# The last 256 rows' recurrence by ScalarE's silu alone, last products by row tile, and new dates for the tail

## Chip, cores and metric

One core of one Trainium2 chip. The metric is the device time of one execution in microseconds (us), the median of several runs. TensorE (PE) multiplies matrices, VectorE (DVE) and GpSimd (POOL) do elementwise work, ScalarE (ACT) evaluates functions, and SyncE (SP) issues most transfers. Each engine works through its own instructions in order; an instruction waits at the head of its engine's queue until what it needs is there, and everything behind it waits too.

## The reference, cut to what matters

```
x = builder_state + mha(layernorm(builder_state), layernorm(base_state))   # 4096 rows, 3202 keys, 8 heads of 64
U = (layernorm(x) @ W_in.T + b_in) @ Bmat                                   # 64 states per row
def step(s, u_t):
    s = silu(s @ A.T) + u_t
    return (s, s)
_, states = scan(step, 0, U)                                                # 4096 steps, one behind the other
out = x + states @ Cmat + mod                                               # mod: one row, the same for all
```

All tensors are float32. The attention is nearly all of the arithmetic; the recurrence over 4096 rows is little work, but each step needs the one before.

## The kernel before

**Attention.** The 4096 query rows are cut into 8 blocks of 512, each with 4 pairs of heads and 2 halves of 256 queries: 64 units. A unit takes 13 steps over pairs of key chunks: scores on PE, exponentials ("weights") on ScalarE, sums of weights on VectorE, products with the values on PE. The last block takes its four first halves before its four second halves, so that the last unit ends the second half of the last 512 rows: the last 256 rows of the sequence.

**The recurrence.** It is contractive, so it is run in pieces from guessed starts, and the kernel compares at the end whether neighbouring pieces agree (to 2^-21 of the largest state); if any does not, a branch at the end (`attend`, line 2410 on) computes everything again step by step. For the rows before the last 256, two sweeps (`sweep`, line 1931) go over 256 pieces of 16 rows: sweep "a" during the last units of attention, from zero, to find starts, and sweep "b" after it, from those starts. One step of a sweep is: PE adds A times the last state to prepared terms (`z_`), ScalarE takes tanh of half of it (`tanh_`), VectorE multiplies (1 + tanh) with it (`h_`), which is twice its silu. All states are kept doubled, and the matrix `a_t` is halved for that (line 962). After each step of sweep b GpSimd adds the inputs (`states`), PE multiplies with Cmat (`products`, two parts of 256 columns), VectorE or ScalarE and GpSimd add the result to rows fetched from memory (`outputs`), and SP stores the rows; 16 steps store all but the last 256 rows.

**The last 256 rows** (`last_rows`, line 2078) come from the last unit. For two row tiles g of 128 rows: output products of the attention (`last_products`, into the PSUM pair `yb`), adding the residual (`l.x1`), mean and variance (`l.stats`), the power -1/2 on GpSimd (`l.factors`), normalising (`l.scaled`), transposing (`l.turn`, `l.copy`), the inputs U (`l.inputs`, `l.kept`); GpSimd adds the modulation row (`l.mod`). Then PE prepares the terms of all pieces (`l.terms`), and a chain of 20 steps follows (line 2191), 16 of them to warm up and 4 that count, each over 32 pieces of 4 rows in each of two halves of the partitions:

```
plan.add(("l.z", t), "PE", 150, partial(on_, t), [("l.h", t - 1)], d, [], [], "quarters")
plan.add(("l.tanh", t), "ACT", 180, partial(tanh_, t), [("l.z", t) if t else "l.terms"], d)
plan.add(("l.h", t), "DVE", 180, partial(h_, t), [("l.tanh", t)], d)
```

Line 1920 is every matmul with `a_t`, line 2158 the tanh of this chain, line 2161 its product, lines 1948 and 1955 tanh and product of the sweeps. After the chain `l.states` (line 2170) adds the inputs, `l.ys` (line 2212) multiplies with Cmat, `last_output` (line 2215) adds to the rows and issues the two last stores, one from SP and one from ScalarE.

**What sets the order.** Each piece of work is given to a planner (`Plan`, line 66) with its engine, an assumed cost in ns, the pieces it comes after, buffers it takes from rings and gives back, and a due date. `order` (line 131) plays the engines forward and, whenever one is free, takes the ready piece with the earliest date; that fixes each engine's instruction order before the kernel is built. The table `SHIFT` (line 93) moves the date of each sort of piece by so many steps of 2150 ns; a name with `.l` stands for that sort in the last two units. Pieces of cost 0 ("start", "py1", "close") only allocate buffers. PSUM here: the ring "s" has two slots of two banks, used by scores, then by the last unit's denominators (`pd_last`, line 1280), the terms of sweep b (`ready_scan`, line 2056) and one of the two pairs of output products (`ready_py`, line 2065).

Of the kernel before, what the change touches and what calls it, by code (L numbers as in the profile page):

```python
# [20 lines left out]
P = 128  # L21
# [54 lines left out]
class Plan:  # L76
# [16 lines left out]
    SHIFT = {  # L93
        "row.store": -0.5, "fold": 17, "rows.outs": 10.25, "heads": -12, "spread": 1.75, "query.flip": -11,
        "states": -5, "inverse": 14.75, "extra": 10, "scale": -55.75, "rest": 11, "row.mod": -20,
        "joined0": -6.25, "b": 1, "add.l": -23, "l.stats": -34.25, "last": -4.5, "base": -34.75,
        "inverse.l": -35, "rows.inputs": 6, "maximum": -13.75, "fall": -19, "query.stats": -4, "den": 6.5,
        "row.scaled": 16, "l.h": -11, "row.stats": -21.25, "rows.turn": 13, "query.scaled": 7.5, "l.mod": -0.5,
        "close": -10, "swap": -2.25, "products": -9, "gather.l": -8, "l.ys": -10, "fall.l": -2, "weights": -3.5,
        "rows.s": 2, "l.x1": 1, "l.kept": 6, "tq": 20, "l.store": -2, "row.move3": 11, "l.from": -5,  # L100
        "l.copy": -12, "l.states": -8, "l.turn": -4, "row.flip": 3.75, "swap.l": -18, "l.near": 4,
        "differ": 12.25, "row.load": 12, "add": -6, "rest.l": -8, "den.l": 11.5, "query.factors": 16,
        "sevenths": -6, "l.z": -2, "scale.l": -0.5, "outs": -3, "output": -12, "query.move3": 3, "number": 0.25,
        "l.inputs": -4, "q": -12, "sums": -4, "row.move2": 2, "row.move1": -0.25, "query.move0": 1.5,
        "stored1": -12, "counted": 1, "to": 12, "sums.l": 9, "row.kept": 8, "so": 10.75, "stored0": 2,
        "l.scaled": -0.25, "row.move0": 4, "rise": -1, "join": -12, "sample": 3.5, "l.idle": 11.75,
        "risen": -0.5, "c2": 1, "yb": 2, "query.load": 8, "query.move2": -4, "row.row": -0.5,
    }
# [112 lines left out]
def xattn_ssm_kernel(  # L221
# [1055 lines left out]
    def sums(w):  # L1277

        if w["last"]:
            w["pd"] = ps_s.tile([P, 2, 512], F32, tag="s", name="pd_last")[:, 0, :QU]  # L1280
            for b in range(2):
                for a in range(2):
                    nc.tensor.matmul(
                        w["pd"][a * HD : (a + 1) * HD],
                        ones,
                        rows_of(w, w["acc"][:, a, b, :], True),
                        start=(b == 0),
                        stop=(b == 1),
                        skip_group_check=True,
                    )  # L1290
            return
# [32 lines left out]
    def finish(w, i, d, plan):  # L1324
# [568 lines left out]
    def open_scan():  # L1893

        t = qp.tile([P, 2, QB], F32, tag="q", name="c2")[:, 0]
# [11 lines left out]
        for name, n in (  # L1907
            ("end0", NCK + 1), ("end1", NCK + 1), ("ul", PRE + 1 + P), ("hw", P), ("hl", P),
            ("sl", P + 1), ("df", NCK), ("thl", P // LT), ("st", P // LT),
            ("top", 1), ("bad", 1), ("badl", 1), ("badr", 1),  # L1910
        ):
            sv[name] = two[:, at_ : at_ + n]
            at_ += n
        assert at_ <= 1024

    def on_a(z, right, **how):

        for v in range(2):
            r = slice(v * NS, (v + 1) * NS)
            nc.tensor.matmul(z[r], a_t[r, r], right[r], stop=True, skip_group_check=True, **how)  # L1920

# [9 lines left out]
    def sweep(k, start, end, d=0, pace=0, after=()):  # L1931
# [32 lines left out]
        for j in range(L):  # L1964
# [100 lines left out]
    def ready_py():  # L2065

        yb = ps_s.tile([P, 2, H], F32, tag="s", name="py")
        sv["py"] = [None, [yb[:, v, :] for v in range(2)]]

# [8 lines left out]
    def last_rows(plan, d):  # L2078
# [75 lines left out]
        def on_(t):  # L2154
            on_a(z_(t), hs_(t - 1), start=False)

        def tanh_(t):
            nc.scalar.activation(sv["thl"], z_(t), AF.Tanh, scale=0.5)

        def h_(t):  # L2160
            nc.vector.scalar_tensor_tensor(hs_(t), sv["thl"], 1.0, z_(t), ALU.add, ALU.mult)

        def from_():

            nc.vector.tensor_tensor(
                sv["st"], sv["hw"][:, LT - 1 :: LT], sv["ul"][:, PRE :: LT][:, : P // LT], ALU.add
            )

        def states_():
            nc.vector.tensor_tensor(sv["sl"][:, 1:], sv["hl"], sv["ul"][:, PRE + 1 :], ALU.add)  # L2170
# [127 lines left out]
    def drain(plan):  # L2298
# [16 lines left out]
        for p in sweep("a", None, "end1", a0 + 1000, A_PACE, ["open"]):  # L2315
            plan.add(*p)
        plan.add("start", "DVE", 0, ready_scan, ["fetch", ("sums", n)], d - 2 * STEP, ["s"])
        plan.add("yb", "DVE", 0, ready_rows, [("den", n - 1, 1)], a0, ["m", "m"])
        plan.add("py1", "DVE", 0, ready_py, ["start", ("rise", n)], d, ["s"])
        for c in range(NC - 1):  # L2320
            i = units.index((NQB - 1, c, 1))
            plan.add(("last", c), "PE", 1900, partial(last_products, c),
                     ["yb"] + [("scale", i, t) for t in range(2) if ("scale", i, t) in plan.pieces] + ([("last", c - 1)] if c else []), d + 8 * STEP + c)
        for j in range(L):
# [245 lines left out]
    with tc.If(n > 0, label="general"):  # L2570
# [14 lines left out]
        with tc.For_i(0, 2 * P // LT, 1):  # L2585
            sl, th, h = sv["sl"], sv["thl"], sv["hw"][:, : P // LT]
            for j in range(LT):
# [70 lines left out]
```

## Time and profile before

| | |
|---|---|
| median of 3 runs | 1905.65 us (1905.32 to 1907.46) |
| the profiled execution | 1904.96 us, span 1903.1 us |
| granted TensorE clock, mean | 0.999 |
| last attention product ends | about 1847.5 us |
| sweep b, first tanh to last product | 1857.8 to 1889.9 us |
| chain over the last 256 rows | 1867.3 to 1894.9 us |
| last store issued | 1898.3 us |

A row of the timeline gives the start from the start of the span, the duration, engine, line of the kernel, operation, output and inputs, and, in square brackets, how long the engine had been idle before it and what ended that. Times are us. In rows that group instructions a mean in ns follows the busy time. PEld is the load of weights into TensorE.

### The profile page before, as it was taken

Reading aid. Unit: us, or ns where it says so; the run is one execution under the profiler, and the core shown is the slowest. Engines: PE = TensorE matmul, PEld = TensorE weight load, DVE = VectorE, ACT = ScalarE, POOL = GpSimd, SP = SyncE. Lnnn points to the kernel's source line nnn. Section 1 sums busy time; section 2 is a strip of 40 time slices with the busy share of each in tenths; the row PEclk is TensorE's granted clock in tenths of the full one; section 3 lists DMA queues with packets and bytes.
Section 4 is the critical chain, followed back from the end, with each engine's and each line's share of the span. In section 5 each row is a group of like instructions: output and inputs, shape, how many; then the busy total and the mean of one; then the engine's idle time right before and its main releaser. Section 6 shows DMA issues by size and latency. Waiting matters only on the chain.

```text
span 1903.1 us, 68781 instructions
## 1 busy us (share of the span) xinstructions
PE 1886.3 (99%) x29632; PEld 1382.5 (73%) x29632; DVE 1547.7 (81%) x2133; ACT 1176.0 (62%) x1675; POOL 254.6 (13%) x386
## 2 busy tenths in 40 slices
PE   9999999999999999999999999999999999999997
PEld 5887678777777777777777777777777777777674
DVE  6642699788979898799978897889978997988776
ACT  3242677575767577657757576757766676757553
POOL 6120300022000300022002200031002200120005
PEclk9999999999999999999999999999999999999999
DMA  8554233133323342223413332334322341546476
GB/s 255 157 158 119 60 103 92 40 112 91 95 73 105 93 113 85 85 69 103 117 39 115 91 100 75 104 86 112 94 70 77 108 110 43 171 115 184 133 199 211
DMA packets 260769, 207.55 MB, mean 109 GB/s; under 512 B 94633, under 2 KB 233897, under 8 KB 260461
## 3 DMA queue, kind: packets, MB, share of 16 engines
q1 hardware_dynamic: 256440, 196.48, 36.0%
q10 hardware_dynamic: 4020, 6.62, 1.1%
q8 instruction: 235, 3.85, 0.9%
q14 instruction: 74, 0.60, 0.1%
HBM read 156.32 MB, written 29.88 MB: 98 GB/s over the span
## 4 chain that ended last, share of the span: by engine, by line


## 5 line engine op out<-in xcount | busy, mean ns | idle before, releaser
L1210 ACT ACTIVATE p<-s,shifts 128x1024 f32<-128x1024 f32 (+1 forms) x832 | 895.1, 1082 | 459.1 <-PE s L1132 442.6
L1218 DVE TENSOR_TENSOR acc<-p,acc 128x1024 f32<-128x1024 f32 (+1 forms) x704 | 836.9, 1189 | 110.0 <-ACT p L1210 85.2
L1268 PE MATMUL po<-p,v 64*64 64x256 f32 x12800 | 851.2, 377 | 1.3 <-DVE o L1322 0.9
L1132 PE MATMUL s<-q,k 64*64 64x256 f32 x12800 | 851.9, 377 | 0.3 <-ACT p L1210 0.2
L1132 PEld LDWEIGHTS s<-q,k 64*64 64x64 f32 x12800 | 505.9, 133 | 198.1 <-ACT p L1210 12.9
L1268 PEld LDWEIGHTS po<-p,v 64*64 64x64 f32 x12800 | 504.4, 133 | 173.3 <-issue 7.8
L1620 POOL TENSOR_TENSOR xr<-xr,rowb 128x512 f32<-128x512 f32 x28 | 35.4, 1274 | 842.5 <-DVE acc L1218 619.7
L1345 DVE RECIPROCAL rd<-rd 128x256 f32<-128x256 f32 (+1 forms) x64 | 109.9, 1719 | 9.6 <-ACT rd L1340 9.6
L1218 DVE TENSOR_TENSOR acc<-p,p 128x1024 f32<-128x1024 f32 x64 | 78.1, 1220 | 26.8 <-ACT p L1210 26.8
L1711 POOL TENSOR_TENSOR xr<-x,modb 128x512 f32<-128x512 f32 x28 | 35.5, 1276 | 197.5 <-DVE acc L1218 155.5
L1242 DVE TENSOR_TENSOR acc<-swap,acc 64x256 f32<-64x256 f32 x126 | 56.1, 446 | 1.7 <-ACT swap L1237 0.2
L1203 DVE TENSOR_TENSOR acc<-x,acc 2x256 f32<-2x256 f32 x128 | 54.9, 429 | 1.4
L1407 POOL TENSOR_SCALAR rstd_x<-mv_x 128x1 f32<-128x1 f32 x28 | 18.9, 676 | 269.7 <-DVE mv_x L1404 268.0
L1237 ACT COPY swap<-acc 64x256 f32<-64x256 f32 x126 | 50.9, 404 | 3.0
L1557 ACT ACTIVATE q<-qx,bias 128x256 f32<-128x256 f32 x42 | 17.6, 471 | 56.8 <-PE qx L392 56.8
L570 DVE TENSOR_TENSOR ks<-pky,ks 128x512 f32<-128x512 f32 x15 | 10.4, 692 | 43.6 <-PE pky L392 28.7
L564 ACT ACTIVATE ks<-pkx,bias 128x256 f32<-128x256 f32 x40 | 16.8, 471 | 44.1 <-PE pkx L392 32.7
L1225 DVE TENSOR_TENSOR acc<-acc 128x512 f32<-128x512 f32 x63 | 42.9, 681 | 0.4
L1322 DVE TENSOR_TENSOR o<-po,o 128x256 f32<-128x256 f32 x64 | 26.9, 420 | 9.3 <-ACT o L1318 9.2
L1340 ACT ACTIVATE rd<-pd 128x128 f32<-128x128 f32 x126 | 33.7, 276 | 0.5 <-PE pd L1296 0.3
L1415 ACT ACTIVATE xh_y<-x,nm_y,rstd_y 128x512 f32<-128x512 f32 x30 | 24.2, 808 | 13.0 <-POOL nm_y L1409 13.0
L1166 DVE TENSOR_REDUCE m<-sm 128x1 f32<-128x256 f32 x64 | 23.7, 411 | 10.1 <-PE sm L1152 10.1
(307 smaller groups left out, 1752.1 us busy)
## 6 DMA issues: line engine op xcount, KB each, us to landing
k<-kd SPq DMA_DIRECT2D x432, 128.0 KB, 2.2
v<-vd SPq DMA_DIRECT2D x432, 128.0 KB, 2.2
xn<-x SPq DMA_DIRECT2D x448, 32.0 KB, 1.9
xr<-in_x_dram SPq DMA_DIRECT2D x30, 256.0 KB, 4.0
x1d<-xr SPq DMA_DIRECT2D x30, 256.0 KB, 2.7
x<-in_x_dram SPq DMA_DIRECT2D x28, 256.0 KB, 2.9
cx<-in_ctx_dram SPq DMA_DIRECT2D x25, 256.0 KB, 4.7
kd<-ks SPq DMA_DIRECT2D x20, 256.0 KB, 2.3
```

The source lines that it names most:

```text
L1132: nc.tensor.matmul(s[k0 : k0 + HD, a, b, :], kts[(*w["at"][:2], c)][r, b * CK + k0 : b * CK + k0 + HD], q[r], start=True, stop=True, skip_ ...
L1203: made = nc.vector.tensor_tensor(to[r], t[r], to[r], ALU.add)
L1210: nc.scalar.activation(t[:, :, :nb, :], w["ps"][c][:, :, :nb, :], AF.Exp, bias=w["shift"])
L1218: return nc.vector.tensor_tensor(w["acc"][:, :, :nb, :], t[:, :, :nb, :], before[:, :, :nb, :], ALU.add)
L1225: return nc.vector.tensor_tensor(acc[:, :, 0, :], acc[:, :, 0, :], acc[:, :, 1, :], ALU.add)
L1237: nc.scalar.copy(w["swap"][r], of[(1 - k) * HD : (2 - k) * HD])
L1242: made = nc.vector.tensor_tensor(of[r], w["swap"][r], of[r], ALU.add)
L1268: nc.tensor.matmul(w["po"][k][a * HD : (a + 1) * HD, :QU], vts[Q, hp, c][r, b, a * HD : (a + 1) * HD], t[r, a, b, :], start=(c == 0 and b ...
L1340: nc.scalar.activation(to, of, AF.Copy, accum_out=rises[:, 3 * i + k : 3 * i + k + 1])
L1345: nc.vector.reciprocal(w["rd"][:, part], (w["pd"] if last else w["rd"])[:, part])
L1620: return nc.gpsimd.tensor_tensor(xs[half][:, t], xs[half][:, t], rowb, ALU.add)
L1711: return nc.gpsimd.tensor_tensor(xt[:, t], x1[:, t], modb, ALU.add)
```

## The change

It has four parts. The chain over the last 256 rows calls `Silu` on ScalarE directly, so that its VectorE product goes; its states are then not doubled inside the chain, so its steps multiply by a second matrix `a2`, twice `a_t`, made once by VectorE, and the two later sums take the chain's result times two. A piece "table" calls silu once on one column, after the last weights. The products of `last_products` are pieces by row tile for all four pairs of heads instead of only the last. The last denominators share their PSUM pair with the output products, "start" comes after the last scores instead of after the last sums, and `sums` of the last unit comes after "start". Some of the planner's costs and dates are new, nearly all of them of pieces in the tail.

The new dates in `SHIFT`, in steps: states -5 to -17, b 1 to -1, l.mod -0.5 to 7.5, l.store -2 to 10, l.turn -4 to 4, l.z -2 to 1, gather.l -8 to -4, fall.l -2 to -2.5, sums.l 9 to 1, rise -1 to 3, rows.outs 10.25 to 10.5; and, with none before, added -12, l.terms 13, joined1 2. The diff without them, and without the fallback's use of another scratch tile:

```
     def sums(w):
         if w["last"]:
-            w["pd"] = ps_s.tile([P, 2, 512], F32, tag="s", name="pd_last")[:, 0, :QU]
+            sv["pd"] = ps_s.tile([P, 2, H], F32, tag="s", name="pd_last")
+            w["pd"] = sv["pd"][:, 0, :QU]
...
-            plan.add(("sums", i), "PE", 880, partial(sums, w), [("add", i, NDC - 1)], d + 1000, ["s"], acc)
+            plan.add(("sums", i), "PE", 880, partial(sums, w), [("add", i, NDC - 1), "start"], d + 1000, ["s"], acc)
...
-            plan.add(("rise", i), "DVE", 480, rise, inverses, d + 9000, [], [("s", ("sums", i))])
+            plan.add(("rise", i), "DVE", 480, rise, inverses, d + 9000)
...
-        sv["c2"] = t
+        sv["c2"], sv["a2"] = t, c2[:, 1, :P]
+        nc.vector.tensor_scalar(sv["a2"], a_t, 2.0, None, ALU.mult)
...
-                    (k, "tanh", j), "ACT", 280, partial(tanh_, j),
+                    (k, "tanh", j), "ACT", 240, partial(tanh_, j),
-                yield (k, "h", j), "DVE", 290, partial(h_, j), [(k, "tanh", j)] + free, d + 800, [], gives
+                yield (k, "h", j), "DVE", 210, partial(h_, j), [(k, "tanh", j)] + free, d + 800, [], gives
...
         def on_(t):
-            on_a(z_(t), hs_(t - 1), start=False)
-        def tanh_(t):
-            nc.scalar.activation(sv["thl"], z_(t), AF.Tanh, scale=0.5)
+            on_a(z_(t), hs_(t - 1), sv["a2"], start=False)
         def h_(t):
-            nc.vector.scalar_tensor_tensor(hs_(t), sv["thl"], 1.0, z_(t), ALU.add, ALU.mult)
+            nc.scalar.activation(hs_(t), z_(t), AF.Silu)
...
         def states_():
-            nc.vector.tensor_tensor(sv["sl"][:, 1:], sv["hl"], sv["ul"][:, PRE + 1 :], ALU.add)
+            nc.vector.scalar_tensor_tensor(
+                sv["sl"][:, 1:], sv["hl"], 2.0, sv["ul"][:, PRE + 1 :], ALU.mult, ALU.add
+            )
+        def table_():
+            nc.scalar.activation(sv["st"][:, :1], neg_half, AF.Silu)
...
-                     [("scale", n, g), ("last", NC - 2)], d + g)
+                     [("scale", n, g), ("last", NC - 2, g)], d + g)
...
-            plan.add(("l.tanh", t), "ACT", 180, partial(tanh_, t), [("l.z", t) if t else "l.terms"], d)
-            plan.add(("l.h", t), "DVE", 180, partial(h_, t), [("l.tanh", t)], d)
+            plan.add(("l.h", t), "ACT", 150, partial(h_, t), [("l.z", t) if t else "l.terms"], d)
+        plan.add("table", "ACT", 1500, table_, [("weights", n, NDC - 1), "c2"], d)
...
-        plan.add("start", "DVE", 0, ready_scan, ["fetch", ("sums", n)], d - 2 * STEP, ["s"])
+        plan.add("start", "DVE", 0, ready_scan, [("scores", n, NDC - 1)], d - 2 * STEP, ["s"])
-        plan.add("py1", "DVE", 0, ready_py, ["start", ("rise", n)], d, ["s"])
+        plan.add("py1", "DVE", 0, ready_py, ["start", ("rise", n)], d)
...
-            plan.add(("last", c), "PE", 1900, partial(last_products, c),
+            for g in range(2):
+                plan.add(("last", c, g), "PE", 950, partial(last_products, c, [g]),
```

More of the change, by code (lines that the diff above doesn't have):

```diff
@@ L93 @@
     SHIFT = {
-        "row.store": -0.5, "fold": 17, "rows.outs": 10.25, "heads": -12, "spread": 1.75, "query.flip": -11,
-        "states": -5, "inverse": 14.75, "extra": 10, "scale": -55.75, "rest": 11, "row.mod": -20,
-        "joined0": -6.25, "b": 1, "add.l": -23, "l.stats": -34.25, "last": -4.5, "base": -34.75,
+        "row.store": -0.5, "fold": 17, "rows.outs": 10.5, "heads": -12, "spread": 1.75, "query.flip": -11,
+        "states": -17, "inverse": 14.75, "extra": 10, "scale": -55.75, "rest": 11, "row.mod": -20,
@@ L97 @@
+        "joined0": -6.25, "b": -1, "add.l": -23, "l.stats": -34.25, "last": -4.5, "base": -34.75,
         "inverse.l": -35, "rows.inputs": 6, "maximum": -13.75, "fall": -19, "query.stats": -4, "den": 6.5,
-        "row.scaled": 16, "l.h": -11, "row.stats": -21.25, "rows.turn": 13, "query.scaled": 7.5, "l.mod": -0.5,
-        "close": -10, "swap": -2.25, "products": -9, "gather.l": -8, "l.ys": -10, "fall.l": -2, "weights": -3.5,
-        "rows.s": 2, "l.x1": 1, "l.kept": 6, "tq": 20, "l.store": -2, "row.move3": 11, "l.from": -5,
@@ L101 @@
-        "l.copy": -12, "l.states": -8, "l.turn": -4, "row.flip": 3.75, "swap.l": -18, "l.near": 4,
+        "row.scaled": 16, "l.h": -11, "row.stats": -21.25, "rows.turn": 13, "query.scaled": 7.5, "l.mod": 7.5,
+        "close": -10, "swap": -2.25, "products": -9, "gather.l": -4, "l.ys": -10, "fall.l": -2.5,
+        "weights": -3.5, "rows.s": 2, "l.x1": 1, "l.kept": 6, "tq": 20, "l.store": 10, "row.move3": 11,
+        "l.from": -5, "l.copy": -12, "l.states": -8, "l.turn": 4, "row.flip": 3.75, "swap.l": -18, "l.near": 4,
@@ L106 @@
-        "l.scaled": -0.25, "row.move0": 4, "rise": -1, "join": -12, "sample": 3.5, "l.idle": 11.75,
-        "risen": -0.5, "c2": 1, "yb": 2, "query.load": 8, "query.move2": -4, "row.row": -0.5,
+        "stored1": -12, "counted": 1, "to": 12, "sums.l": 1, "row.kept": 8, "so": 10.75, "stored0": 2,
+        "l.scaled": -0.25, "row.move0": 4, "rise": 3, "join": -12, "sample": 3.5, "l.idle": 11.75,
+        "risen": -0.5, "c2": 1, "yb": 2, "query.load": 8, "query.move2": -4, "row.row": -0.5, "added": -12,
@@ L108 @@
+        "l.terms": 13, "joined1": 2,
     }
@@ L1914, in open_scan, with on_a @@
         assert at_ <= 1024
-    def on_a(z, right, **how):
+    def on_a(z, right, a=a_t, **how):
         for v in range(2):
             r = slice(v * NS, (v + 1) * NS)
-            nc.tensor.matmul(z[r], a_t[r, r], right[r], stop=True, skip_group_check=True, **how)
+            nc.tensor.matmul(z[r], a[r, r], right[r], stop=True, skip_group_check=True, **how)
     def terms(z, q, start):
@@ L2065, in ready_py @@
     def ready_py():
-        yb = ps_s.tile([P, 2, H], F32, tag="s", name="py")
-        sv["py"] = [None, [yb[:, v, :] for v in range(2)]]
+        sv["py"] = [None, [sv["pd"][:, v, :] for v in range(2)]]
     def last_products(c, tiles=range(2)):
```

18 lines of the change are left out of this document (10 added, 8 removed).

## The prediction

> **What bounds the kernel now.** I read the page's busy line first, then the table of windows over the last 64 us, then the timeline of single engines inside it.
>
> ```profile
> span 1903.1 us, 68781 instructions
> PE 1886.3 (99%) x29632; PEld 1382.5 (73%) x29632; DVE 1547.7 (81%) x2133; ACT 1176.0 (62%) x1675; POOL 254.6 (13%) x386
> ```
>
> TensorE is busy for 99% of the span, and the change touches no matmul of the attention. So it can only pay where TensorE does not set the pace. Columns of the windows: length, then busy time of PE, PEld, DVE, ACT, POOL, then clock, DMA share, GB/s.
>
> ```profile
> 1851.00:1856.00 5.00, 5.00 (x18) 2.09 (x18) 3.20 (x9) 0.00 (x0) 0.00 (x0) 1.00 1.04 253
> 1856.00:1867.00 11.00, 9.24 (x114) 5.92 (x112) 8.35 (x20) 2.92 (x8) 6.96 (x9) 1.00 0.58 175
> 1867.00:1895.00 28.00, 23.98 (x362) 14.57 (x354) 20.62 (x60) 11.70 (x44) 17.41 (x22) 1.00 0.73 246
> 1895.00:1899.00 4.00, 1.49 (x10) 0.55 (x10) 2.73 (x9) 0.42 (x2) 0.42 (x1) 0.86 0.50 176
> ```
>
> Up to 1856 TensorE is full. After that no engine is: in 1867 to 1895 VectorE works 20.62 of 28 us, ScalarE 11.70, and even PE's modelled 23.98 counts overlapping latencies. Two chains of dependent small steps run there: the second sweep (16 steps, "b") and the chain over the last 256 rows (20 steps, "l"). The l chain ends last:
>
> ```profile
> 1867.28 0.19 ACT L2158 ACTIVATE scan<-zl 128x32 f32<-128x32 f32 x1
> 1867.50 0.21 DVE L2161 SCALAR_TENSOR_TENSOR scan<-scan,zl 128x32 f32<-128x32 f32 x1 [0.75 <-ACT scan L2158]
> ...
> 1882.53 0.21 DVE L2161 SCALAR_TENSOR_TENSOR scan<-scan,zl 128x32 f32<-128x32 f32 x1 [0.81 <-ACT scan L2158]
> 1882.79 0.32 PE L1920 MATMUL zl<-scan,a_t 64*64 64x32 f32 x4 [0.47 <-DVE scan L2161]
> 1883.15 0.20 ACT L2158 ACTIVATE scan<-zl 128x32 f32<-128x32 f32 x1
> 1883.57 0.20 DVE L2161 SCALAR_TENSOR_TENSOR scan<-scan,zl 128x32 f32<-128x32 f32 x1
> ...
> 1893.97 0.19 ACT L2158 ACTIVATE scan<-py_o 128x32 f32<-128x32 f32 x1
> 1894.72 0.20 DVE L2161 SCALAR_TENSOR_TENSOR scan<-scan,py_o 128x32 f32<-128x32 f32 x1
> 1894.95 0.62 DVE L2170 TENSOR_TENSOR scan<-scan 128x128 f32<-128x128 f32 x1
> 1898.33 0.37 ACTq L2219 DMA_DIRECT2D out_dram<-xr_l  x1
> ```
>
> From the last product at 1894.72 to the end of the span at 1903.1 lie 8.4 us of states, output products, output rows and the last transfer, which the change leaves as they are.
>
> **The chain of 20 steps, the main term.** One step is PE, then ScalarE's tanh, then VectorE's product, then PE again. I call the time from the start of tanh to the start of the product the hop. The change removes it: silu takes the place of tanh and feeds PE itself. The first hop is 0.22 us and the last 0.75; the 20 of them, read off between the two rows quoted first and last, add up to 9.1 us. Eight are undisturbed at 0.22 to 0.23 (1867.28 to 1867.50); in the others the product stood behind output rows or the b chain's product in VectorE's order. The floor is 20 x 0.225 = 4.5 us; the other 4.6 us are queueing on VectorE.
>
> Silu's own time is not in this trace. The nearest row is the tanh on the same operands, 0.19 to 0.20 us; I take that, with 0 to +0.1 us a step as bounds (+2 us in all), since only the function differs. Nor is the release of PE by ScalarE in this chain; the nearest rows are these:
>
> ```profile
> 11.30 0.81 ACT L317 ACTIVATE xh_c<-cx,nmr_c,rstd_c 128x512 f32<-128x512 f32 x1 [3.48 <-POOL nmr_c L309]
> 12.17 0.42 PEld L333 LDWEIGHTS tp_c<-ident,xh_c 128*128 128x128 f32 x4 [0.64 <-ACT xh_c L317]
> ```
>
> ScalarE ends at 12.11, PE loads at 12.17: 0.06 us. VectorE's release is the same: 1882.53 + 0.21 = 1882.74, PE at 1882.79. So the hop goes whole.
>
> How much of the 4.6 us of queueing comes back as a gain? From product to next tanh the 19 other parts take (1893.97 - 1867.28) - (9.1 - 0.75) = 18.3 us, 0.96 each, where an undisturbed one takes 0.62 (1882.53 to 1883.15). So PE and ScalarE, in order too, already hold the chain by 19 x 0.34 = 6.5 us, and a step that arrives earlier meets these queues. I take half of it: **-6.8 us**, bounds -4.5 and -9.1 (with the slower silu -2.5).
>
> **The front of the chain.** The last products are split by row tile and the modulation rows ("l.mod") are dated later.
>
> ```profile
> 1850.36 5.42 PE L2073 MATMUL yb<-wo,o 128*128 128x512 f32 x12
> 1855.03 0.69 DVE L2094 TENSOR_TENSOR x_l<-yb,xr_l 128x512 f32<-128x512 f32 x1 [1.77 <-PE yb L2073]
> 1855.71 0.44 PE L1920 MATMUL z<-scan,a_t 64*64 64x128 f32 x4
> 1855.98 1.67 PE L1920 MATMUL z<-u,a_t 64*64 64x384 f32 x8
> 1856.78 0.69 DVE L2094 TENSOR_TENSOR x_l<-yb,xr_l 128x512 f32<-128x512 f32 x1
> 1859.28 0.54 DVE L2106 TENSOR_SCALAR xh_yl<-x_l,mv_yl,rstd_yl 128x512 f32<-128x512 f32 x1
> 1860.19 2.68 POOL L2136 TENSOR_TENSOR xr_l<-x_l,modb 128x512 f32<-128x512 f32 x2
> 1860.26 1.49 DVE L2106 TENSOR_SCALAR xh_yl<-x_l,mv_yl,rstd_yl 128x512 f32<-128x512 f32 x1 [0.25 <-POOL rstd_yl L2102]
> 1864.99 0.36 DVE L2129 TENSOR_SCALAR scan<-py_o,bu 64x128 f32<-64x128 f32 x1
> 1865.38 1.11 PE L1920 MATMUL zl<-scan,a_t 64*64 64x128 f32 x16
> ```
>
> The split lets row tile 0 have all its products before tile 1, but the chain's terms (1865.38) need both tiles, and tile 1's products still end when the 5.42 us of PE end, at 1855.78; its rows started at 1856.78, so at most 1.0 us is there. The normalising of tile 1 took 1.49 us beside the modulation on GpSimd and 0.54 without it: moving that away gives 0.95. Against it, the b sweep is dated two steps (4.3 us) earlier and no longer waits for the last unit's sums. Its opening is 0.44 + 1.67 = 2.1 us of PE, and if it goes ahead of the last products, in the window where PE is full (5.00 of 5.00), it pushes them by as much. Bounds -1.95 and +2.1; I take **0**, the middle.
>
> **The b sweep.** Its rows must be out before the kernel ends.
>
> ```profile
> 1857.76 0.28 ACT L1948 ACTIVATE scan<-z 128x128 f32<-128x128 f32 x1 [9.85 <-PE z L1920]
> ...
> 1889.60 0.28 DVE L1955 SCALAR_TENSOR_TENSOR scan<-scan,z 128x128 f32<-128x128 f32 x1
> 1894.83 0.96 SPq L2019 DMA_DIRECT2D out_dram<-row  x2
> ```
>
> Its last store is issued by 1895.79, the l chain's by 1898.70: 2.9 us of slack. If l gains 6.8, b must come 3.9 us earlier. Sixteen steps took 32.1 us, 2.0 each, so b is full of waits as well. It gets up to 4.3 us of earlier start, and VectorE loses 20 x 0.21 = 4.2 us of work in its way. Half of each is 4.2 us, which just suffices (2.9 + 4.2 = 7.1). As two uncertain limits stand side by side, I take 1 us off the sum.
>
> **What costs nothing, and why.** The doubled matrix is one more VectorE instruction, near this row (0.28 us), issued with the load of Cmat long before the tail; VectorE's adds there lie beside PE's 99%. If the ring buffer it writes is late, VectorE's queue waits behind it and PE after that: at most one 1.2 us add, bound +1.2.
>
> ```profile
> L2043 DVE TENSOR_SCALAR scan<-scan 128x128 f32<-128x128 f32 x1 | 0.3, 277 | 0.0
> L1067 ACT ACT_TABLE_LOAD x1 | 1.3, 1283 | 1.8 <-issue 1.8
> L1948 ACT ACTIVATE scan<-z 128x128 f32<-128x128 f32 x12 | 3.3, 277 | 3.2 <-PE z L1920 3.1
> ```
>
> A load of function tables is in this trace once, at the start: 1.283 us. The change calls silu once on its own after the last weights, so one load more falls there; ScalarE stood idle 9.85 us before 1857.76, which hides it (uncovered: +1.3). The sums of old products as two-times-plus keep their instruction count; sharing one PSUM pair between denominators and products takes away a wait for a ring slot before 1857 and adds "start" ahead of the sums, a bookkeeping step without an instruction. The other dates reorder the last two units and the b outputs; I price them inside the bounds above.
>
> **Sum.** -6.8 + 0 + 1 = -5.8 us. The profiled execution took 1904.96 us, 1.86 outside its span, 0.69 under the median shown; the same step from the median 1905.65 gives **1899.9 us**.
>
> **Rivals.** *The stores become the end.* The l chain gains in full but b keeps its place; then only the slack of 2.9 us shows: 1902.8. For it: b's steps carry every store; against it: the freed VectorE. Chance 0.16.
>
> *The wait moves to PE's order.* The chain's terms are dated 13 steps later and silu steps queue behind products and b's steps; the hop's floor of 4.5 us is won, and the b opening's 2.1 lost at the front: 1903.2. For it: 6.5 us of such queueing now. Chance 0.12, with silu slow as the same case.
>
> *Slower: table loads inside the chains.* The b sweep keeps tanh, 12 of its activations lie among l's 20 in 1866 to 1896 (row above). If no one table set held both functions, each would mean a load before and one after: 24 x 1.283 = 30.8 us, so 1930.7. It decides from 8 loads on (5.8 + 3.8 over 1.283). Against it: tanh, exp, copies and abs live here under one load. Chance 0.04.
>
> The Trainium skill, "ScalarE: Activation LUTs", section "Table sets: the hidden batching unit", says that functions come in named sets, lists tanh beside exp, and does not list silu with either; the 1283 ns it gives for a load agree with the row, and with its drain (2.66 us a switch, an estimate) the rival would cost 64 us. The Trainium skill, "SBUF — State Buffer", section "SBUF: two separate sides", calls the port pair that VectorE and GpSimd share an exclusive lock; the 1.49 against 0.54 us agrees, and by that rule silu on ScalarE is out of its reach.
>
> *Slower: the fallback.* The kernel compares neighbouring states to 2^-21 and redoes everything if they differ. The l chain would be silu's and its neighbour tanh's; if their errors differ by more, the time is beyond 3,000 us, since the redo holds all the attention that fills the 1903.1 us. Nothing here shows it. Chance 0.03.
>
> **How the numbers follow.** A measurement can tell about 0.2% from no change, 3.8 us: faster means under 1901.8. The forecast has 0.64, with its own range 1894.6 (-9.1 - 1.95) to 1901.8; what gains less belongs to the first two rivals, which are "same" with 0.28. The two slow ones and 0.01 of a front more than 3.8 us later are "slower". The range reaches from 1895.0 to 1905.0, leaving out about 0.15.
>
> **What would show it.** The profile after should have no VectorE product among the l steps, one more table load before 1857, steps of 0.62 us where undisturbed and about 1.14 on average (1867.3 to 1889 in 19 parts), terms near 1865.4, and the last l activation near 1889. The front fails if terms start after 1867; the stores rival is right if the last row store is issued after the last output rows; the table rival if loads stand between the chains.

## The result and the profile after

The changed kernel takes **1901.71 us** (median of 13 runs, 1901.12 to 1902.63), the kernel before 1905.76 us on the same chip (13 runs, 1904.55 to 1908.09): ratio **0.9978**, 95% interval [0.9969, 0.9986]: 0.2% faster, which is clear of the noise. The forecast was 1899.9 us. The profiled execution took 1901.72 us, its span 1899.8, which is 3.3 us under the span before.

The page of the changed kernel, its head and busy line, and below them the table of windows with the four windows of before:

```profile
span 1899.8 us, 68757 instructions
PE 1884.8 (99%) x29632; PEld 1383.5 (73%) x29632; DVE 1545.2 (81%) x2114; ACT 1178.1 (62%) x1677; POOL 253.5 (13%) x386
```

```profile
1851.00:1856.00 5.00, 5.00 (x19) 2.12 (x19) 3.99 (x11) 0.00 (x0) 0.39 (x1) 1.00 1.05 276
1856.00:1867.00 11.00, 9.24 (x95) 5.28 (x94) 7.34 (x18) 3.55 (x9) 7.59 (x10) 1.00 0.57 180
1867.00:1895.00 28.00, 23.65 (x382) 16.11 (x380) 19.32 (x47) 12.06 (x44) 16.74 (x21) 0.98 0.76 254
1895.00:1899.00 4.00, 0.00 (x0) 0.00 (x0) 0.00 (x1) 0.00 (x0) 0.00 (x0) 0.50 0.40 146
```

VectorE has 13 instructions fewer in 1867 to 1895 (47 against 60), and after 1895 no engine has work that shows (before: 2.73 us of VectorE). TensorE is full up to 1856 in both. So the time came out of the tail. Its timeline begins with the **front**: last products, x_l, turns and inputs, kept, terms.

```profile
1849.90 5.42 PE L2076 MATMUL yb<-wo,o 128*128 128x512 f32 x12
...
1855.25 0.43 PE L1924 MATMUL z<-scan,a_t 64*64 64x128 f32 x4
...
1855.46 0.69 DVE L2097 TENSOR_TENSOR x_l<-yb,xr_l 128x512 f32<-128x512 f32 x1
...
1858.42 0.67 DVE L2109 TENSOR_SCALAR xh_yl<-x_l,mv_yl,rstd_yl 128x512 f32<-128x512 f32 x1 [0.47 <-POOL rstd_yl L2105]
...
1859.45 1.09 PE L2125 MATMUL pu_l<-xn_l,wc 128*64 128x128 f32 x8
...
1860.47 0.66 PE L2115 MATMUL py_o<-ident,xh_yl 128*128 128x128 f32 x4
...
1861.06 0.33 PE L1924 MATMUL z<-scan,a_t 64*64 64x128 f32 x2
...
1864.78 0.36 DVE L2132 TENSOR_SCALAR scan<-py_o,bu 64x128 f32<-64x128 f32 x1
...
1868.43 0.39 PE L1924 MATMUL z<-scan,a_t 64*64 64x128 f32 x4
...
1868.64 1.04 PE L1924 MATMUL zl<-scan,a_t 64*64 64x128 f32 x16
```

x_l of the second tile is 1.3 us earlier than before (1855.46 against 1856.78), 0.46 of it because the last products started that much earlier; its normalising takes 0.67 us instead of 1.49. But kept moves only from 1864.99 to 1864.78. About half of what was won goes at the second tile's turn (1860.47), which stands on PE behind the first tile's inputs (1859.45); the other half goes between turn and kept (4.3 us instead of 3.1), where the second tile's inputs stand behind products of b on PE and kept behind a product of b on VectorE. Then the last kept is done at 1865.14, and the terms start 3.5 us later, at 1868.64, behind products and two steps of b on PE. Before, they started at 1865.38, right after kept.

The start of the tail varies from execution to execution: in e5 and e11 below, whose order up to there is the changed kernel's, the same x_l starts at 1856.09 and at 1854.66. Times of two traces are therefore compared here as lengths where it matters; a difference of less than about 1 us in absolute time alone shows nothing.

The **chain and the end**, the same timeline further on:

```profile
1869.73 0.24 ACT L2161 ACTIVATE scan<-zl 128x32 f32<-128x32 f32 x1 [0.23 <-PE zl L1924]
...
1878.12 0.22 ACT L2161 ACTIVATE scan<-zl 128x32 f32<-128x32 f32 x1
...
1878.39 0.32 PE L1924 MATMUL zl<-scan,c 64*64 64x32 f32 x4 [0.37 <-ACT scan L2161]
...
1878.75 0.23 ACT L2161 ACTIVATE scan<-zl 128x32 f32<-128x32 f32 x1 [0.27 <-PE zl L1924]
...
1890.57 0.22 ACT L2161 ACTIVATE scan<-py_o 128x32 f32<-128x32 f32 x1
1890.71 0.69 DVE L2018 SCALAR_TENSOR_TENSOR row<-pd_last,row 128x512 f32<-128x512 f32 x1 [1.12 <-ACT y_l L2012]
1890.75 1.27 POOL L2015 TENSOR_TENSOR row<-y_l,row 112x512 f32<-112x512 f32 x1 [1.71 <-ACT y_l L2012]
1891.31 0.86 DVE L2171 SCALAR_TENSOR_TENSOR scan<-scan 128x128 f32<-128x128 f32 x1
...
1894.98 0.37 ACTq L2225 DMA_DIRECT2D out_dram<-xr_l  x1
```

The product is gone: silu starts at 1878.12, PE goes on 0.05 us after its end (its weights are `a2`, which the profile calls c after the tile that holds it), and the next silu starts 0.63 us after the first. The chain lasts 21.06 us (1869.73 to 1890.79), before 27.64 (1867.28 to 1894.92). The states (L2171) wait until 1891.31 behind a row add on VectorE that waited for ScalarE's y_l, and take 0.86 us beside GpSimd's row add. They end at 1892.17, 0.15 us after that GpSimd add. So it was before, where they end at 1895.57, 0.15 us after this one:

```profile
1894.15 1.27 POOL L2011 TENSOR_TENSOR row<-y_l,row 112x512 f32<-112x512 f32 x1 [2.86 <-ACT scan L2158]
```

What differs is how soon GpSimd's add ends after the chain: 0.50 us before, 1.23 after the change.

The **b sweep**, its first tanh, last product and row stores, and the one load of function tables in the tail:

```profile
1843.73 1.28 ACT L2176 ACT_TABLE_LOAD   x1
...
1857.29 0.28 ACT L1952 ACTIVATE scan<-z 128x128 f32<-128x128 f32 x1 [9.82 <-PE z L1924]
...
1884.98 0.28 DVE L1959 SCALAR_TENSOR_TENSOR scan<-scan,z 128x128 f32<-128x128 f32 x1
...
1887.52 4.84 SPq L2023 DMA_DIRECT2D out_dram<-row  x6
```

b starts 0.5 us earlier, as the last products do, and ends 4.6 us earlier: 28.0 us instead of 32.1. The last row store is issued by 1892.36, the l chain's rows by 1895.35.

### The profile page after: what moved, and what is told of

Its sections match the earlier page's. It is cut to its first block, busy times and chain, and to the rows that moved or that the text cites. A ratio compares the mean times of both kernels' runs of the same rounds, so it can differ in the third digit from the quotient of the medians.

```text
span 1899.8 us, 68757 instructions
## 1 busy us (share of the span) xinstructions
PE 1884.8 (99%) x29632; PEld 1383.5 (73%) x29632; DVE 1545.2 (81%) x2114; ACT 1178.1 (62%) x1677; POOL 253.5 (13%) x386
## 4 chain that ended last, share of the span: by engine, by line
## 5 line engine op out<-in xcount | busy, mean ns | idle before, releaser
L1324 DVE TENSOR_TENSOR o<-po,o 128x256 f32<-128x256 f32 x64 | 26.9, 421 | 8.8 <-ACT o L1320 8.7
```

## The experiments

Theory from the profile after: silu shortens the l chain, and the dates do not save anything; they hand b a better place on TensorE at the l chain's cost, so that the row stores do not become the end. Rivals: silu alone gives the gain; the rest without silu gives it; b is faster because VectorE is freer; the split of the last products carries it. The table gives the runs first: times and ratio to the kernel before, run beside it, and, from the timeline of each profiled execution, b's last product (start), chain (first l activation, length), and when the last row store and the last l row were issued (start plus duration). The shared PSUM pair, the new costs and the dates other than b's, l.terms' and the output pieces' have no run of their own.

| run | median us | ratio, 95% | b's last product | l chain | row stores | l rows |
|---|---|---|---|---|---|---|
| before | | | 1889.60 | 1867.28 + 27.6 | 1895.8 | 1898.7 |
| changed | 1901.71 | 0.9978 [0.9969, 0.9986] | 1884.98 | 1869.73 + 21.1 | 1892.4 | 1895.4 |
| e1, silu, old dates | 1906.59 | 1.0001 [0.9992, 1.001] | 1892.47 | 1867.93 + 19.4 | 1898.3 | 1891.2 |
| e2, all but silu | 1910.88 | 1.0022 [1.0013, 1.0031] | 1883.70 | 1869.00 + 30.7 | 1892.0 | 1903.9 |
| e7, all but the dates | 1905.07 | 0.9997 [0.9988, 1.0006] | 1891.91 | 1866.21 + 20.8 | 1897.7 | 1890.6 |
| e10, b's date old | 1904.08 | 0.9989 [0.998, 0.9998] | 1891.30 | 1866.36 + 20.0 | 1896.7 | 1890.0 |
| e11, output dates old | 1901.89 | 0.9979 [0.997, 0.9988] | 1884.20 | 1868.93 + 21.1 | 1891.6 | 1894.6 |
| e4, terms early | 1902.59 | 0.9979 [0.997, 0.9988] | 1884.58 | 1866.59 + 21.0 | 1895.1 | 1892.7 |
| e5, e4 and ys late | 1902.11 | 0.9979 [0.997, 0.9988] | 1885.62 | 1867.64 + 21.0 | 1894.3 | 1894.0 |
| e9, last products whole | 1900.52 | 0.9971 [0.996, 0.9982] | 1883.83 | 1869.27 + 20.4 | 1891.3 | 1894.2 |

### e1: silu alone, on the kernel before

```
-            nc.vector.scalar_tensor_tensor(hs_(t), sv["thl"], 1.0, z_(t), ALU.add, ALU.mult)
+            nc.scalar.activation(hs_(t), z_(t), AF.Silu)
```

with `a2`, the sums with two-times-plus and the table piece that belong to it; dates, costs, split and PSUM as before.

> The kernel before with silu in the chain (second matrix, table call and the two sums by two with it), and nothing else of the change: old dates, old last products, old PSUM sharing. Theory (the hop that went is the gain, whatever the dates): the chain of 20 steps takes 20 to 23 us instead of 27.6, starts near 1867, and the kernel gains 2 to 4 us on the kernel before, held by the row stores of the second sweep, which ended 2.9 us ahead. Rival (the new dates are the gain): the chain stays at 25 us or more and the time within 1 us of the kernel before.

No change in time, though the chain is 8.3 us shorter; 2 to 4 us were expected. The timeline of e1: b's opening on PE goes ahead of the last products, x_l starts at 1857.32, and SP issues the row stores behind everything else.

```profile
1852.75 1.68 PE L1922 MATMUL z<-u,a_t 64*64 64x384 f32 x8
...
1854.37 3.70 PE L2075 MATMUL yb<-wo,o 128*128 128x512 f32 x8
...
1857.32 0.69 DVE L2096 TENSOR_TENSOR x_l<-yb,xr_l 128x512 f32<-128x512 f32 x1 [2.19 <-PE yb L2075]
...
1890.20 0.35 SPq L2225 DMA_DIRECT2D out_dram<-xr_l  x1
...
1890.65 7.66 SPq L2021 DMA_DIRECT2D out_dram<-row  x7
```

The l rows go out 7.5 us earlier than before, the row stores 2.5 us later; they are the end now. It is the first rival of the prediction, in a kernel without the dates, and worse than that rival had it: b doesn't keep its place, its last product comes 2.9 us later than before.

### e2: everything but silu

```
-            nc.scalar.activation(hs_(t), z_(t), AF.Silu)
+            nc.scalar.activation(sv["thl"], z_(t), AF.Tanh, scale=0.5)
...
+            nc.vector.scalar_tensor_tensor(hs_(t), sv["thl"], 1.0, z_(t), ALU.add, ALU.mult)
```

> The kernel after with the old chain (tanh on ScalarE, product on VectorE, states doubled) and all else of the change kept. Theory: the chain is 26 to 28 us long again, starts where it does after the change (about 1869.7), and the time is 0 to 3 us above the kernel before, since the late start is not paid back. Rival (dates): the kernel keeps at least 2 us of its 4 us gain.

The split, the shared pair, the costs and the dates are all kept. 4.3 us slower than before, more than expected. Here b is as fast as in the changed kernel (its last product starts at 1883.70), with all 20 products of the l chain still on VectorE: **the freed VectorE isn't what speeds b.** The l chain pays: 30.7 us, where 26 to 28 were expected.

### e7: everything but the dates

```
-        "states": -17, "inverse": 14.75, "extra": 10, "scale": -55.75, "rest": 11, "row.mod": -20,
-        "joined0": -6.25, "b": -1, "add.l": -23, "l.stats": -34.25, "last": -4.5, "base": -34.75,
+        "states": -5, "inverse": 14.75, "extra": 10, "scale": -55.75, "rest": 11, "row.mod": -20,
+        "joined0": -6.25, "b": 1, "add.l": -23, "l.stats": -34.25, "last": -4.5, "base": -34.75,
...
-        "l.terms": 13, "joined1": 2,
```

> The kernel after with the old table of dates, all else of the change kept (silu, products by row tile, shared PSUM, new costs). Theory, from the run with silu alone: the l chain ends early but the sweep's rows late, the last row store after 1895, the time within 2 us of the kernel before. Rival (the structure, not the dates, gives the 4 us): at least 3 us below the kernel before.

All dates of the tail are the old ones again (an excerpt above). The split, the shared PSUM pair and silu together gain 0.7 us (1905.78 to 1905.07), inside the uncertainty: as in e1 the rows are last, issued by 1897.7 against 1890.6 of the l rows. So silu with the rest needs the dates, and (e2) the rest, dates and all, needs silu. New dates in the kernel before, and nothing else, were not run. The chain is 20.8 us long here, 21.1 with the new dates and 19.4 in e1.

### e10 and e11: which of the dates

e10 takes back one date, e11 those of the output pieces:

```
-        "joined0": -6.25, "b": -1, "add.l": -23, "l.stats": -34.25, "last": -4.5, "base": -34.75,
+        "joined0": -6.25, "b": 1, "add.l": -23, "l.stats": -34.25, "last": -4.5, "base": -34.75,
```

```
-        "states": -17, "inverse": 14.75, "extra": 10, "scale": -55.75, "rest": 11, "row.mod": -20,
+        "states": -5, "inverse": 14.75, "extra": 10, "scale": -55.75, "rest": 11, "row.mod": -20,
...
-        "risen": -0.5, "c2": 1, "yb": 2, "query.load": 8, "query.move2": -4, "row.row": -0.5, "added": -12,
-        "l.terms": 13, "joined1": 2,
+        "risen": -0.5, "c2": 1, "yb": 2, "query.load": 8, "query.move2": -4, "row.row": -0.5,
+        "l.terms": 13,
```

> The changed kernel with b's own date moved from -1 back to 1, so that the b sweep stands two steps later in the plan, everything else as changed. If b's earlier place is what makes its rows ready sooner, the last product of b ends 1 to 2 us later than 1885.3, the last row store is issued as much later than 1892.4, and, as the last l rows are issued at 1894.4 to 1895.0, the time moves by 0 to 1 us (1901.7 to 1902.7). If the date only sets who goes first on TensorE around 1853, the second x_l write comes earlier and the l chain with it by up to 1 us, at the same time.

> The changed kernel with the old dates of the output pieces alone: states at -5, no dates for added and joined1. TensorE's order stays as it is, only the order of the row adds, joins, state products and stores on GpSimd, VectorE and SyncE differs. If the dates of the output pieces give b its faster pace, b's last product comes 2 to 5 us after 1885.3 and the last row store 2 to 4 us after 1892.4, behind the l rows, and the time is 1903 to 1905. If the pace comes from the order on TensorE, b's last product stays within 0.5 us and the time within 0.5 us of 1901.7.

e11 behaves like the changed kernel: the output dates do nothing that can be measured. e10 takes 2.2 us more than e11, run beside it, more than either theory expected. b's first tanh stays at 1857.36 (changed: 1857.29), so the date doesn't move its start; its last product moves from 1884.98 to 1891.30. What moves is the order on TensorE. From the end of one of b's products to the start of the matmuls that follow from it, the 15 waits add up to 4.0 us in the changed kernel, 10.0 in e10 and 8.4 before; the rest of b, 23.7 to 24.2 us, is the same in the three. In e10 b's third step stands behind eight of b's own output products until 1861.60 (changed: 1861.06). All kernels with b's new date but e8, with its loads, have a b of 26.9 to 28.5 us, all with the old one 32.1 us or more. In the changed kernel 7 of b's 16 tanh come before the first l activation, in e10 and before only 4, but this lead isn't the cause: in e4 and e5 below it is 5, and b takes 28.0 us there too (waits in e4: 4.2).

The l chain is 4.4 us earlier in e10 (it ends at 1886.36), but that is of no use, as the last group of row stores, in SP's timeline, ends at 1896.7:

```profile
1861.60 0.27 PE L1924 MATMUL z<-scan,a_t 64*64 64x128 f32 x1
...
1891.41 5.26 SPq L2023 DMA_DIRECT2D out_dram<-row  x6
```

So b's date decides how long b waits in TensorE's order, and the time follows the chain that ends later.

### e4 and e5: the terms early

e4 takes the date of l.terms back; e5 also holds `l.ys` on TensorE behind the last products of b's rows.

```
-        "l.terms": 13, "joined1": 2,
+        "l.terms": 0, "joined1": 2,
...
-        plan.add("l.ys", "PE", 1200, partial(last_ys, "a"), ["l.states"], d, ["mt"])
+        plan.add("l.ys", "PE", 1200, partial(last_ys, "a"), ["l.states"] + [("products", L - 1, part) for part in range(2)], d, ["mt"])
```

> The kernel after with the date of the chain's terms moved back by 13 steps to where it was before. Theory: the terms start near 1865.5 instead of 1868.6, the first silu near 1867, and the kernel ends 1 to 2.5 us earlier than the kernel after, as the chain keeps about 21 us. Rival (PE's order gives and takes): the second sweep falls behind by as much, the chain grows longer beside it, and the time stays within 1 us of the kernel after or is worse.

> The chain's terms dated as before (the edit of e4_terms_early) and, besides, the last output products of the 256 rows made to come after the second sweep's last products on PE. In e4_terms_early the l chain was done 2.2 us earlier against the front than after the change, but half of the last products of the sweep stood behind the output products on PE and the last row store was issued at 1895.1. Theory (the end is the later of the l rows and the last row store, plus about 4.8 us): the last row store goes out near 1893 and the l rows near 1892.5, so 1.5 to 2.5 us less than the kernel after, 5.5 to 6.5 less than before. Rival (something else follows the front): within 0.7 us of the kernel after.

In e4 the terms start at 1865.51, 0.8 us after kept instead of 3.5, and the first silu at 1866.59: the date was what held them back, for 2.7 us. The l rows are issued 2.7 us earlier (0.4 of it because this execution reached the tail earlier), but half of b's last products now stand behind `l.ys`, and the last row store comes after the l rows:

```profile
1889.24 0.66 PE L2218 MATMUL py_a<-c,scan 64*128 64x512 f32 x1 [0.58 <-DVE scan L2171]
...
1890.95 0.66 PE L1998 MATMUL pd_last<-c,scan 64*64 64x256 f32 x8
...
1891.71 0.45 SPq L2225 DMA_DIRECT2D out_dram<-xr_l  x1
1894.14 0.95 SPq L2023 DMA_DIRECT2D out_dram<-row  x2
```

No gain. e5 puts that right: row stores and l rows are issued by 1894.3, 1.1 us before the changed kernel's last. Still no gain, against my expectation. Its profiled execution is the slowest of its runs (1903.37 us), so its end must be read with care; the windows of the last microseconds (last columns: DMA share, GB/s), the changed kernel's first and then three of e5's, show why:

```profile
1890.00:1894.00 4.00, 2.58 (x20) 1.50 (x18) 2.61 (x8) 1.14 (x4) 1.27 (x1) 1.00 0.93 306
1894.00:1895.00 1.00, 0.05 (x3) 0.00 (x0) 1.00 (x3) 0.00 (x0) 0.00 (x0) 0.55 0.26 92
1895.00:1896.00 1.00, 0.00 (x0) 0.00 (x0) 0.00 (x1) 0.00 (x0) 0.00 (x0) 0.50 0.77 289
1896.00:1897.00 1.00, 0.00 (x0) 0.00 (x0) 0.00 (x0) 0.00 (x0) 0.00 (x0) 0.50 0.64 240
```

```profile
1894.00:1895.00 1.00, 0.21 (x4) 0.10 (x4) 0.15 (x1) 0.00 (x0) 0.00 (x0) 1.00 1.02 320
1895.00:1896.00 1.00, 0.00 (x0) 0.00 (x0) 0.00 (x0) 0.00 (x0) 0.00 (x0) 1.00 1.04 315
1896.00:1897.00 1.00, 0.00 (x0) 0.00 (x0) 0.00 (x0) 0.00 (x0) 0.00 (x0) 0.93 0.93 291
```

In e5 the transfers are full until 1897: what is issued together has to share about 320 GB/s. In the changed kernel the rows' data is nearly through by 1894, and the l rows have the path to themselves.

### e12: e5 without the last row stores

```
-        yield "stored0", "SP", 350, partial(stored, 0), "joined0"
-        yield "stored1", "SP", 350, partial(stored, 1), "added" if spread else "joined1"
+        if j < 12 or k_all:
+            yield "stored0", "SP", 350, partial(stored, 0), "joined0"
+            yield "stored1", "SP", 350, partial(stored, 1), "added" if spread else "joined1"
```

`k_all` is a new argument of `outputs` that is False here.

> The kernel of e5 with the row stores of the last four steps of the sweep left out, so their output rows are not written; all arithmetic is still done. If the transfers at share 1.0 in 1894 to 1897 hold the end back in e5, the l rows, issued near 1893.0 and 1893.6, now land in the 3 us or so that a lone store takes, and the time is 1899.0 to 1900.5 against 1902.1 of e5. If the end goes by the issue of the l rows plus a fixed 4.8 us whatever else is under way, it is 1901.0 to 1902.0.

1899.49 us (1898.53 to 1900.16), ratio 0.9966 [0.9954, 0.9978], against 0.9979 for e5: about 2.5 us less with the same chain. (e5 was not run beside it; e11, which was, took 1901.89.) Windows of e12:

```profile
1890.00:1894.00 4.00, 2.05 (x14) 0.96 (x14) 3.60 (x11) 0.82 (x2) 1.27 (x1) 1.00 0.13 50
1894.00:1895.00 1.00, 0.00 (x0) 0.00 (x0) 0.03 (x1) 0.00 (x0) 0.00 (x0) 1.00 0.87 324
1895.00:1896.00 1.00, 0.00 (x0) 0.00 (x0) 0.00 (x0) 0.00 (x0) 0.00 (x0) 1.00 0.00 0
```

The l rows, issued by 1893.6, are through by 1895. So in e5 transfers are the third limit, behind the l chain and b: there both chains end at once.

### e3: the states first

The last joined0 and added pieces of b are planned behind `l.states`, so that the states no longer stand behind the row add.

```
+                if j == L - 1 and sort in ("joined0", "added"):
+                    more = more + ["l.states"]
```

> The kernel after, with the last two row sums of the second sweep (VectorE's and GpSimd's of step 15) placed behind the sum that makes the last states. Theory: after the change that sum waits 0.5 us behind a row sum on VectorE and then runs 0.86 us beside GpSimd's row sum instead of 0.3; with them behind it the last output rows go out 0.8 to 1.1 us earlier than the 1894.98 of the kernel after, and the end follows, since the row stores had 2.6 us of slack. Rival (the row stores decide the end): no gain or a loss of up to 1 us.

1901.71 us, ratio 0.9976 [0.9966, 0.9986]: nothing gained. The states start right after the chain, but beside GpSimd's row add, and last as much longer as they waited in the changed kernel:

```profile
1890.09 1.26 POOL L2015 TENSOR_TENSOR row<-y_l,row 112x512 f32<-112x512 f32 x1 [1.71 <-ACT y_l L2012]
1890.16 1.33 DVE L2171 SCALAR_TENSOR_TENSOR scan<-scan 128x128 f32<-128x128 f32 x1 [1.24 <-ACT scan L2161]
```

They end 0.14 us after GpSimd's add, as in the changed kernel and before. Only half of the edit took effect: the plan orders each engine's own work, and GpSimd's add, which needs nothing of the states, started when its y_l was there. So VectorE's row add in front of the states costs nothing; GpSimd's add sets when they end. What the kernel gains with that add behind the states wasn't measured.

### e6 and e8: the table of functions

e6 leaves the piece "table" out. e8 adds an exponential of one column behind each tanh of b, to see what a load costs between the chains.

```
-        plan.add("table", "ACT", 1500, table_, [("weights", n, NDC - 1), "c2"], d)
```

```
+            if k == "b":
+                nc.scalar.activation(sv["badl"], neg_half, AF.Exp)
```

> The kernel after without the single early call of silu. The load of tables of 1.28 us then falls on the first silu of the chain. Theory (that chain is the end): terms unchanged, first silu 0.5 to 1.3 us later, the end later by as much, since ScalarE waited 0.23 us for PE there. Rival (the load hides in waits of the chain): no change.

> The kernel after with an exp on one scratch column behind each tanh of the second sweep. Theory of the price named in the prediction: where silu and exp alternate on ScalarE each change costs a load of 1.28 us; with about 13 sweep steps among the 20 silu steps 20 to 26 loads appear and the time rises by 15 to 33 us over the kernel after. Rival (loads hide in ScalarE's idle time, 15 of 27 us there): less than 8 us.

e6: 1901.93 us, 0.9979 [0.997, 0.9988]. The load now stands in front of the first silu (1868.94), which comes at 1870.24; the chain ends at 1890.80. Counted from the second tile's x_l (1854.89 in e6), the first silu is 1.1 us later than in the changed kernel and the end of the chain 0.6 us, as expected; in the time that is too little to be told from no change. e8: 1921.99 us (two runs), 1.0082 [1.0064, 1.0101], 20 us more. Groups of e8's tail:

```profile
L1954 ACT ACT_TABLE_LOAD x10 | 12.8, 1283 | 0.2
L2163 ACT ACT_TABLE_LOAD x10 | 12.8, 1283 | 0.2
L1952 ACT ACTIVATE scan<-z 128x128 f32<-128x128 f32 x16 | 4.4, 276 | 12.6 <-PE z L1924 12.6
```

Twenty loads, each where silu follows exp (L2163) or exp follows silu (L1954). b's tanh (L1952) stands behind exp or behind silu without one, so it goes with either. Twenty loads of 1.283 us and 16 exponentials of 0.2 us cost 20 us together, so a load between the chains costs 1.0 us at most.

### e9: the last products whole

```
-            for g in range(2):
-                plan.add(("last", c, g), "PE", 950, partial(last_products, c, [g]),
+            plan.add(("last", c), "PE", 1900, partial(last_products, c),
...
```

> The changed kernel with the last products of the final chunk issued as one 1.9 us group for both row tiles again, everything else as changed. If the split is worth what its rows say, the first row tile's x_l write starts about 1.3 us later (1855.0 instead of 1853.7) and the second at its place (1855.5 to 1856.8); kept of the first tile moves from 1860.6 towards 1862 to 1864, the first l activation stays at 1869.7 because l.terms stands behind b's z on TensorE, and the time is 1901.7 to 1902.3. If the split carries the gain, the chain itself starts 1 to 2 us later and the time is 1903 to 1904.

It is the fastest of the kernels that write all rows, outside both expected ranges: 1900.52 us (1900.14 to 1900.90), while e11, the changed kernel but for output dates without effect, took 1901.89 (1900.94 to 1902.39) beside it. The timeline of e9:

```profile
1856.28 0.69 DVE L2097 TENSOR_TENSOR x_l<-yb,xr_l 128x512 f32<-128x512 f32 x1
...
1859.57 0.43 PE L1924 MATMUL z<-scan,a_t 64*64 64x128 f32 x4
...
1864.48 0.36 DVE L2132 TENSOR_SCALAR scan<-py_o,bu 64x128 f32<-64x128 f32 x1
...
1868.19 1.04 PE L1924 MATMUL zl<-scan,a_t 64*64 64x128 f32 x16
```

x_l of the second tile is 0.8 us later without the split, inside what was expected, but the first turn now comes behind b's step on PE (1859.57; in the changed kernel that step waited until 1861.06 behind turn and inputs), kept is 0.3 us and the terms 0.45 us earlier, and b ends 1.1 us earlier (the last products start within 0.03 us of the changed kernel's, so the times can be compared). So with these dates the change would be 1.4 us better without its split. Which part of that is the split and which the reshuffled order isn't told apart.

## Why the prediction was right and where it was wrong

The time fell by 4.05 us where 5.8 were forecast, to the edge of the prediction's own case (under 1901.8, where its first two rivals begin). The main term came as forecast; one term put at nothing, the front, did not.

- **The bound: right.** TensorE up to 1856 is as it was; all of the gain lies in the tail.
- **The hop, -6.8: measured -6.6**, undisturbed step 0.63 (forecast 0.62), mean (1890.57 - 1869.73) / 19 = 1.10 (forecast 1.14). Silu took 0.227 us on average instead of 0.196, 0.6 us in 20 steps, inside the bounds. But that taking half of the queueing came out is partly luck. In the kernel before silu takes 8.3 of the 9.1 us (e1): PE's and ScalarE's queues take back 0.8 us, not the 2.3 that I gave them. The rest of the change then makes the chain 1.7 us longer: 1.4 without the dates (e1 to e7, from 19.4 to 20.8), 0.3 by the dates (e7 to changed). With tanh it makes it 3.0 us longer (before to e2), so silu takes 9.6 there (30.67 to 21.06).
- **The front, 0: measured +2.45.** This is the step that failed. The split and the modulation gave at x_l and at the normalising what the rows promised, and b's opening didn't go ahead of the last products (it does so in e1 and e7). But I priced the date of l.terms only inside a rival, not in the sum; e4 shows that the date alone held the terms back for 2.7 us, and of the 2.7 us by which the second normalising ended earlier (1859.09 against 1861.75) 2.4 went again between it and kept.
- **The end part, unchanged: measured +0.8.** From the end of the last product or silu to the issue of the last l row it is 3.41 us before (1894.92 to 1898.33) and 4.19 after (1890.79 to 1894.98): the states wait 0.5 us more behind a row add and take 0.86 instead of 0.62 us. Both come from one thing, GpSimd's last row add, which now ends 1.23 us after the chain instead of 0.50; e3 takes the wait away, and the states last until the same add has ended.
- The three give -6.58 + 2.45 + 0.78 = -3.35, the span's -3.3. The forecast's own sum was -5.8; the 1 us that I took off for two limits side by side wasn't needed in the changed kernel, where the last row store is issued 3 us before the l rows; it made up by luck for a third of the two terms that were missing.
- **b's 4.2 us: measured 4.6** at its last product, by neither of my two reasons. The earlier start is 0.5 us, not half of 4.3, and that is the whole tail's (e10: the date leaves the start alone); the freed VectorE gives nothing (e2). It is the order on TensorE, where b waits 4.0 us instead of 8.4.
- **Stores become the end:** not in the changed kernel, but in e1, e7, e10 and e4. The rival's price, 1902.8, held b at its old place; in e1 and e7 b's last product came 2.9 and 2.3 us later than before, and they took 1906.59 and 1905.07. **The wait moves to PE's order:** the half of it at the front came true (2.45 us, where it had 2.1, and by the date of the terms, not by b's opening); the other half, a chain that wins only the floor of 4.5 us, didn't.
- **Table load hidden, a2 for nothing: right.** One load at 1843.73 in front of idle time; the last products start at 1849.90, 0.46 us earlier than before, which is within what executions differ by, so no delay shows there. **Table loads between the chains: not so**, as tanh is served by silu's load too. The Trainium skill, "ScalarE: Activation LUTs", section "What ACT_TABLE_LOAD costs", gives 1283 ns for a load, and e8 agrees; with the drain that it adds, 20 loads would cost 53 us, an estimate from its 2.66 us a switch, where e8 measured 20, its exponentials included. The fallback didn't happen.

## What to carry to other kernels

Where two chains of small steps share the engines and both have stores at the end, the time goes by the later of the two, and a chain made shorter pays only as far as the order hands what was won to the other: here silu alone gave nothing, everything but silu lost 4.3 us, everything but the dates won 0.7, within the uncertainty, and all together won 4.0. Price the dates of a change as a transfer between chains, each with its own last store, and put them into the sum, not beside it. Then see to the transfers: in e5, where both chains end together, they have to share them.

## What the runs showed of the hardware

Silu took 0.227 us on average for 128x32 (16 instructions), tanh with its scale of 0.5 on the same shape 0.196. In these kernels one load served tanh and silu in turn, and tanh also ran under exp's; between exp and silu a load stood at each change: 1.283 us each, at most 1.0 us of it seen in the time (e8). An add of 128x128 on VectorE took 0.28 to 0.29 us alone (e5 at 1889.85, e2 at 1899.71), and 0.62, 0.86 and 1.33 us beside a GpSimd add of 112x512 (before, changed, e3): in all three it ended 0.14 to 0.15 us after GpSimd's, whenever it had started. Stores at the end ran at 291 to 324 GB/s with a DMA share of 0.87 to 1.04 in the windows shown of e5 and e12, and the span ended 4.1 us (e12) to 5.7 us (e10) after the last store was issued, 7.3 us in e5's profiled execution.
